# Four graph layers on one core: copies of features and rho's first pass on ScalarE, the loads at the part change in another order, W ahead of the features

## The chip, the core and the metric

The kernel runs on one core of a Trainium2 chip. A core has TensorE (matmuls; PE in the profile, PEld for its weight loads), VectorE (DVE), ScalarE (ACT), GpSimd (POOL) and SyncE (SP), each with an instruction queue of its own, and 16 DMA engines that move the transfers issued by SP, ScalarE and GpSimd. Working memory is SBUF, and matmuls write into eight PSUM banks. The metric is the device time of one execution in microseconds; the comparison is made by the median of several runs.

## What is computed

16 samples `x` of 1024 nodes with 256 features, and one adjacency matrix `adj` of 1024 x 1024 with few non-zero elements per row, pass through four layers, all in float32:

```
# layer 0: scored edges
pre_u, pre_v = h @ W1[:d], h @ W1[d:]
S   = sigmoid(relu(pre_u[:, :, None] + pre_v[:, None] + b1) @ W2 + b2)
a_t = einsum('buv,bud->bvd', S * adj, h)
m_t = einsum('uv,bud->bvd', adj, h) * h
z   = beta1 * h + beta2 * (a_t @ Wa + ba) + beta3 * (m_t @ Wm + bm)
# layer 1
z = z + relu(einsum('ij,bjd->bid', adj, z) @ W.T + b)
# layers 2 and 3, each with weights of its own
feats = z @ W1.T
f1    = feats @ W2 + b2
coefs = softmax(leaky_relu(f1[:, :, None] + f1[:, None, :]) + adj)
z     = coefs @ feats + bias2 + z
```

## The kernel before

**Preparation (to about 111 us).** `load_h` loads a sample, `load_w1` the three pieces of W (both halves of W1, and Wa), and eight loads bring the rows of `adj` into `adj_sb`. The order of the issues is that of lines 378 to 384. ScalarE's DMA queue carries two of the four pieces of sample 0 and then W; SP's queue carries the other two pieces, sample 1, adj, samples 2 and 3. TensorE transposes samples 0 to 3 (L300) and multiplies them with W (`edge_sides`), in the order that `first_group` writes out; ScalarE copies the results into `st` (L323, L324), from where they go to u_d, v_d and hw_d in DRAM. Meanwhile VectorE scales Wa by beta2 (L159) and then finds the largest 32 elements of each row of `adj` (L438 to L444). Three small matmuls (L458, L460, L478) count over partitions what it found; the last of its results, `ok`, decides which arm of the kernel runs (L507). With these inputs it is the arm with lists of neighbours.

**First part (to about 956 us).** For each sample, `messages` multiplies it with `adj`, and `without_edges` makes zb, the part of layer 0 that needs no scores, and stores it as zb_d. Beside it run the scores.

**Scores.** `score_steps` is a generator of 8 steps of search and 152 steps for each group of four samples (608 in all). A step gathers 128 rows of v_d (GpSimd, L697, 0.5 MB), adds u (VectorE, L807), applies relu and the weight (VectorE, L809) and sums over the features in four ScalarE activations (L813). The scores go to DRAM by scatters (L702, `dense_d`). `Side.along` drives it: each `yield` of the main work gives a number of microseconds, times `RATE` (0.26 in the first part, 0.255 after), and for each whole one that is owed a score step is issued. So the yields set how much scoring stands between which pieces of main work. A group's products wait until all of its scores are scattered (`while g not in finished`, and the wait of `load_gd`).

**Second part, by groups of four samples.** `with_edges` runs over four column blocks `v` and eight row tiles `ut` in each. A step loads a 0.5 MB block gd of scores (L888, four buffers, SP's queue), ScalarE reorders it into gc (L1066), and TensorE multiplies hw with it (16 matmul instructions) into all eight banks. After each `v` VectorE adds the sums to `z` (L1089). The z tiles of the first group come from zb_d, 1 MB each (`load_z`, L902); its first four gd blocks are loaded ahead, at the end of the first part. In the first group the same loop reloads the transposed adjacency into `adj_sb` (L1081, 0.5 MB for each of eight rows; it is called `ea` from there on) and takes its exponential on ScalarE (`exponential`, L1056). `paced(ins, n)` makes an instruction wait for the product that was issued n products earlier. An SP queue entry that waits holds up all entries behind it.

`pair_layers` then takes two samples through layers 1 to 3. Layer 1 is `layer_one` (L1106, L1116, L1117, L1124). Layers 2 and 3 factor the softmax: `front` makes the features of a sample in eight tiles, each a matmul into one bank and a copy to SBUF (L982); the copy goes through `evacuate`, which takes VectorE (L136) and ScalarE (L138) in turn. There are 32 fronts (16 samples, two layers). `scales` finds the largest logit (L997 to L1011), makes `rho` in two passes (L1013: add the shift and take the positive part, from two banks of 512 columns; L1016: the exponential), `tau` (L1017), and scales the features (L1018, L1020). It isn't issued at once but put on the list `later`, which `catch_up` empties after the second tile of the next front (L983) or after the first tile of the next `sums`. `sums` makes a tile `m` from rho, tau and ea on VectorE (L1038, four buffers) and multiplies it with the features into four banks; VectorE and ScalarE then divide and write back (L1051, L1212, L1223, or L1249, L1253).

The last group has no scores beside it. Its second pair's layer 1 is instead gathered by lists (`far_ahead`, `by_lists`, `from_lists`) while its first pair runs.

The program is recorded line by line, but the layer beneath it may move instructions of one engine past each other where nothing depends on the order.

Of the kernel before, what the change touches and what calls it, by code (L numbers as in the profile page):

```python
# [12 lines left out]
AF = mybir.ActivationFunctionType  # L13
ALU = mybir.AluOpType
AX = mybir.AxisListType
P = 128
# [22 lines left out]
def after(tc, ins, others, kind, why):  # L39
    dep = mybir.DependencyInfo(kind, mybir.DependencyReason.DATA)  # L40
    for o in others:
        tc.add_manual_dep(ins.ins, o.ins.name, dep, reason=why)
# [23 lines left out]
def gnn_stack_kernel(  # L66
# [27 lines left out]
    nc = tc.nc  # L94
    B, N, D = x.shape
    NT = N // P
    DH = D // P
    HN = 512
# [9 lines left out]
    def bank():  # L108
        return psum[-1].tile([P, HN], F32, tag="bank", name="bank")
# [8 lines left out]
    def paced(ins, back=6):  # L118


        if recent:
            after(tc, ins, [recent[max(0, len(recent) - back)]], mybir.DependencyClass.Sync, "keeps pace")
        return ins

    def product(*args, **kw):
        recent.append(nc.tensor.matmul(*args, **kw))  # L126
        del recent[:-BACK]
        return recent[-1]
# [4 lines left out]
    def evacuate(dst, src):  # L133
        turn[0] += 1
        if turn[0] % 2 and not by_scalar[0]:
            nc.vector.tensor_copy(dst, src)  # L136
        else:
            nc.scalar.activation(dst, src, AF.Copy)  # L138
# [12 lines left out]
    def load_w1(pool, queue):  # L151

        w = pool.tile([P, DH, 3, D], F32, name="w1")
        for s, a in enumerate((g0_W1[:D], g0_W1[D:], g0_Wa)):
            queue.dma_start(w[:, :, s, :], a.rearrange("(c p) k -> p c k", p=P))
        return w

    def with_beta2(w):
        return nc.vector.tensor_scalar(w[:, :, 2, :], w[:, :, 2, :], beta2, None, ALU.mult)  # L159
# [112 lines left out]
        flat = dense[i][:DUMP].rearrange("(c p r) b -> c p (r b)", p=P, r=ZERO // GB)  # L272
        return [flat[c] for c in range(flat.shape[0])]

    def load_h(pool, b, pieces=1, other=nc.sync):
        h = pool.tile([P, NT, D], F32, tag="wide", name="h")
        n = NT // pieces
        for t in range(0, NT, n):
            queue = other if t // n % 2 else nc.sync
            queue.dma_start(h[:, t : t + n, :], x[b, t * P : (t + n) * P].rearrange("(t p) d -> p t d", p=P))  # L280
        return h

    def node_pairs(t):
# [81 lines left out]
    with ExitStack() as stack:  # L365
        prep = stack.enter_context(tc.tile_pool(name="prep", bufs=4))
        prep1 = stack.enter_context(tc.tile_pool(name="prep1", bufs=1))
        early = stack.enter_context(tc.tile_pool(name="early", bufs=8))
# [6 lines left out]
                yield 2.4  # L375
                yield from edge_sides(prep, b, w1, hT)

        hs = [load_h(early, 0, pieces=4, other=nc.scalar)]
        w1 = load_w1(prep1, nc.scalar)
        with_beta2(w1)  # L380
        hs.append(load_h(early, 1))
        for t in range(NT):
            nc.sync.dma_start(adj_sb[:, t, :], adj_v[:, t, :])
        hs += [load_h(early, b) for b in range(2, GB)]
# [72 lines left out]
        ps = bank()  # L457
# [219 lines left out]
    with tc.If(listed > 0) as arm:  # L677
        with ExitStack() as stack:
# [197 lines left out]
            def ttile(name):  # L876
                return wide_t.tile([P, TW], F32, tag="wide", name=name)
# [29 lines left out]
            z_loads = []  # L907
# [61 lines left out]
            to_load, to_exp = list(range(NT)), []  # L969

            def front(x, weights):

                wT = weights.wT
                f = ttile("feats").rearrange("p (t d) -> p t d", t=NT)
                for jt in range(NT):
                    ps = bank()
                    for dh in range(DH):
                        product(
                            ps[:, : D + 1], x[:, dh, jt * P : (jt + 1) * P], wT[:, dh, :],
                            start=dh == 0, stop=dh == DH - 1,  # L980
                        )
                    evacuate(f[:, jt, :], ps[:, : D + 1])  # L982
                    if jt == 1:  # L983
                        catch_up()
                    yield 0.86
                made = {}
                later.append(lambda: scales(f, weights, made))
                return made

            def scales(f, weights, made):  # L990


                b2 = weights.b2
                r = two.tile([P, N], F32, tag="rho", name="rho")
                ta = small.tile([P, NT], F32, tag="tau", name="tau")
                top = small.tile([P, 1], F32, tag="top", name="top")
                nc.vector.tensor_reduce(top, f[:, :, D], AX.X, ALU.max)  # L997
                sh = small.tile([P, 4], F32, tag="shift", name="shift")
                banks = []
                for v in range(NV):  # L1000
                    ps = bank()
                    for c in range(HT):
                        jt = v * HT + c
                        nc.tensor.transpose(  # L1004
                            ps[:, c * P : (c + 1) * P], f[:, jt, D : D + 1].to_broadcast([P, P]), ident
                        )
                    banks.append(ps)
                ps = bank()
                nc.tensor.transpose(ps[:, :P], top.to_broadcast([P, P]), ident)
                nc.vector.tensor_reduce(sh[:, 0:1], ps[:, :P], AX.X, ALU.max)  # L1010
                nc.vector.scalar_tensor_tensor(sh[:, 3:4], b2, 2.0, sh[:, 0:1], ALU.mult, ALU.add)  # L1011
                for v in range(NV):
                    nc.vector.tensor_scalar(r[:, v * HN : (v + 1) * HN], banks[v], sh[:, 3:4], 0.0, ALU.add, ALU.max)  # L1013
                nc.vector.tensor_scalar(sh[:, 1:2], sh[:, 0:1], -0.01, None, ALU.mult)
                nc.vector.tensor_scalar(sh[:, 2:3], sh[:, 0:1], -0.99, None, ALU.mult)
                nc.scalar.activation(r, r, AF.Exp, scale=-0.99)  # L1016
                nc.scalar.activation(ta, f[:, :, D], AF.Exp, bias=sh[:, 2:3], scale=0.99)  # L1017
                nc.scalar.activation(f[:, :, D], f[:, :, D], AF.Exp, bias=sh[:, 1:2], scale=0.01)  # L1018
                for jt in range(NT):
                    nc.scalar.activation(f[:, jt, :D], f[:, jt, :D], AF.Identity, scale=f[:, jt, D : D + 1])  # L1020
                made.update(f=f, r=r, ta=ta)
# [3 lines left out]
            def catch_up():  # L1025
                while later:
                    later.pop(0)()
# [27 lines left out]
            def exponential(jt):  # L1055
                paced(nc.scalar.activation(ea[:, jt, :], ea[:, jt, :], AF.Exp), 16)  # L1056

            def with_edges(g, hw, z):

                for v in range(N // QN):  # L1060
                    cols = slice(v * QN, (v + 1) * QN)
                    acc = [[bank() for _ in range(DH)] for _ in range(GB)]
                    for ut in range(NT):
                        gd = first_gd.pop(0) if first_gd else load_gd(g, v, ut, back=BACK)
                        gc = gc_pool.tile([P, GB, QN], F32, tag="gc", name="gc")
                        paced(nc.scalar.activation(gc, gd.rearrange("p n i -> p i n"), AF.Copy), 16)  # L1066
                        for i in range(GB):
                            for eh in range(DH):
                                product(
                                    acc[i][eh][:, :QN], hw[i][:, ut, eh * P : (eh + 1) * P], gc[:, i, :],  # L1070
                                    start=ut == 0, stop=ut == NT - 1,
                                )
                        if z_loads and ut > 1:
                            load, i = z_loads.pop(0)
                            paced(load(i))
                        if (to_load or to_exp) and ut % 2 and not z_loads:
                            if v and to_exp:
                                exponential(to_exp.pop(0))
                            if to_load:
                                jt = to_load.pop(0)  # L1080
                                paced(nc.sync.dma_start(ea[:, jt, :], adjT_d[jt]), 16)  # L1081
                                to_exp.append(jt)
                        yield 3.4
                    if v == N // QN - 1:
                        while to_exp:
                            exponential(to_exp.pop(0))
                    for i in range(GB):
                        for eh in range(DH):
                            nc.vector.scalar_tensor_tensor(  # L1089
                                z[i][:, eh, cols], acc[i][eh][:, :QN], zbias[:, eh : eh + 1], z[i][:, eh, cols],  # L1090
                                ALU.add, ALU.add,
                            )
# [105 lines left out]
            def pair_layers(b, z, ahead, first):  # L1198
# [59 lines left out]


                m0 = yield from front(z[0], gat2)  # L1260
                m1 = yield from front(z[1], gat2)
                yield from sums(m0, 0, second(0))
# [57 lines left out]
    with arm.Else():  # L1320
        with ExitStack() as stack:
# [88 lines left out]
            with tc.For_i(0, B, 1) as b:  # L1410
                h = load_h(wide, b)
# [36 lines left out]
```

## Time and profile before

| | us |
|---|---|
| median of 3 runs (lowest, highest) | 3244.6 (3230.55, 3249.76) |
| profiled execution: its time, the span of its instructions | 3257.53, 3255.8 |
| TensorE busy, by stage (us from the start of the span): | |
| 300 to 900 (first part) | 596.7 of 600 |
| 900 to 1200 (part change, first products) | 279.5 of 300 |
| 1200 to 2600 (second part, groups 0 to 2) | 1352.4 of 1400 |
| 2600 to 3256 (last group) | 626.1 of 656 |
| TensorE clock granted, mean over the span | 0.988 |

The profile lists every instruction with its start and length, and what ended the idle time of its engine before it. A line such as `PE bank L126 <- DVE m L1038` reads: TensorE's instruction of line 126 that writes `bank` waited for VectorE's instruction of line 1038 that writes `m`. All products are issued by a helper, so they share line 126 and are told apart by their tiles. A float32 product appears as two matmul instructions; matmuls are pipelined, and 64 of 256 columns take 14.1 us at full clock. The groups list the mean time of one instruction, and the waits list total, number and longest. `DMA share` is the mean busy share of the 16 engines and can pass 1 where packets overlap. The execution profiled is 13 us slower than the median of the runs.

### The profile page before, as it was taken

Reading aid. Unit: us, or ns where it says so; the run is one execution under the profiler, and the core shown is the slowest. Engines: PE = TensorE matmul, PEld = TensorE weight load, DVE = VectorE, ACT = ScalarE, POOL = GpSimd, SP = SyncE. Lnnn points to the kernel's source line nnn. Section 1 sums busy time; section 2 is a strip of 40 time slices with the busy share of each in tenths; the row PEclk is TensorE's granted clock in tenths of the full one; section 3 lists DMA queues with packets and bytes.
Section 4 is the critical chain, followed back from the end, with each engine's and each line's share of the span. In section 5 each row is a group of like instructions: output and inputs, shape, how many; then the busy total and the mean of one; then the engine's idle time right before and its main releaser. Section 6 shows DMA issues by size and latency. Waiting matters only on the chain. (4 is left out here: it accounts for less than half of the span.)

```text
span 3255.8 us, 39220 instructions
## 1 busy us (share of the span) xinstructions
PE 3132.2 (96%) x12122; PEld 2203.5 (68%) x12122; DVE 2433.7 (75%) x3366; ACT 1880.1 (58%) x6320; POOL 1826.6 (56%) x1483
## 2 busy tenths in 40 slices
PE   8999999999997999999999999999999999999999
PEld 5544544555556678578776867778686678858888
DVE  7787777777775799799668979867898872148754
ACT  3245556566667766566976656688666654413232
POOL 1146888676664666657566666665676550066600
PEclk9999999999998999999999999999999999999999
DMA  8998898879799755656875575587656525475600
GB/s 286 328 323 305 278 288 267 272 226 275 240 322 317 214 162 162 205 154 209 291 226 174 151 221 154 182 286 232 182 151 210 169 90 168 127 246 142 167 15 27
DMA packets 281899, 687.49 MB, mean 211 GB/s; under 512 B 45184, under 2 KB 137344, under 8 KB 274512
## 3 DMA queue, kind: packets, MB, share of 16 engines
q0 software_dynamic: 128224, 387.80, 41.0%
q1 hardware_dynamic: 125472, 245.45, 22.0%
q10 hardware_dynamic: 27984, 51.65, 4.2%
q8 instruction: 97, 1.59, 0.2%
q14 instruction: 122, 1.00, 0.1%
HBM read 553.45 MB, written 131.32 MB: 210 GB/s over the span
## 5 line engine op out<-in xcount | busy, mean ns | idle before, releaser
L813 ACT ACTIVATE z<-z 128x256 f32<-128x256 f32 x2432 | 978.9, 405 | 702.6 <-DVE z L809 613.4
L807 DVE TENSOR_TENSOR z<-z,u 128x1024 f32<-128x1024 f32 x608 | 739.2, 1220 | 402.9 <-PE bank L126 263.0
L126 PE MATMUL bank<-feats,m 128*128 128x257 f32 x4096 | 926.1, 384 | 30.5 <-DVE m L1038 21.7
L697 POOL DMA_INDIRECT z<-v_d,slot_v x512 | 655.1, 1279 | 471.2 <-ACT z L813 241.6
L126 PEld LDWEIGHTS bank<-feats,m 128*128 128x128 f32 x4096 | 768.4, 191 | 160.1 <-DVE m L1038 28.2
L702 POOL DMA_INDIRECT dense_d<-gt,slot_at x512 | 634.1, 1238 | 198.7 <-issue 139.6
L809 DVE SCALAR_TENSOR_TENSOR z<-z,w2r 128x1024 f32<-128x1024 f32 x608 | 737.9, 1220 | 8.5
L126 PE MATMUL bank<-gc,hw 128*128 128x256 f32 x2048 | 459.3, 385 | 33.1 <-ACT gc L1066 28.4
L126 PEld LDWEIGHTS bank<-gc,hw 128*128 128x128 f32 x2048 | 388.4, 192 | 103.4 <-ACT gc L1066 40.5
L813 ACT ACTIVATION_READ_ACCUMULATOR z<-z 128x1 f32 x2432 | 458.2, 188 | 0.0
L126 PE MATMUL bank<-adj_sb,h 128*128 128x512 f32 x1024 | 442.5, 592 | 2.8 <-ACT st L323 2.6
L1038 DVE SCALAR_TENSOR_TENSOR m<-rho,tau,adj_sb 128x512 f32<-128x512 f32 x512 | 374.3, 744 | 69.7 <-PE bank L126 66.2
L126 PE MATMUL bank<-adjT_in,y 128*128 128x512 f32 (+1 forms) x960 | 401.5, 579 | 5.1 <-DMA adjT_in<-adjT_d 2.6
L126 PEld LDWEIGHTS bank<-adj_sb,h 128*128 128x128 f32 x1024 | 194.3, 190 | 243.1 <-issue 237.7
L126 PE MATMUL bank<-w,hT 128*128 128x512 f32 (+1 forms) x1024 | 337.9, 490 | 10.8 <-DMA w<-in_L_gnn_W_dram 8.7
L126 PEld LDWEIGHTS bank<-adjT_in,y 128*128 128x128 f32 x960 | 181.8, 190 | 220.4 <-issue 207.6
L1066 ACT ACTIVATE gc<-gd 128x1024 f32<-128x1024 f32 x128 | 264.6, 2067 | 92.1 <-PE bank L126 53.9
L126 PEld LDWEIGHTS bank<-w,hT 128*128 128x128 f32 x1024 | 195.7, 192 | 154.8 <-issue 131.5
L126 PE MATMUL bank<-g_wT,z 128*128 128x257 f32 x1024 | 235.9, 385 | 1.1 <-DVE z L1117 0.9
L697 POOL DMA_INDIRECT z<-v_d,x_node x96 | 127.7, 1331 | 175.9 <-ACT z L813 108.1
L126 PEld LDWEIGHTS bank<-g_wT,z 128*128 128x128 f32 x1024 | 194.5, 193 | 32.4 <-issue 3.3
L697 POOL DMA_INDIRECT z<-y_d,slot_v x96 | 107.4, 1119 | 62.5 <-DVE msg L1176 41.7
(162 smaller groups left out, 2385.9 us busy)
## 6 DMA issues: line engine op xcount, KB each, us to landing
gd<-dense_d SPq DMA_DIRECT2D x128, 512.0 KB
dense_d<-zero ACTq DMA_DIRECT2D x64, 512.0 KB
adjT_in<-adjT_d SPq DMA_DIRECT2D x112, 256.0 KB
h<-in_x_dram SPq DMA_DIRECT2D x19, 1024.0 KB
u_d<-st SPq DMA_DIRECT2D x64, 256.0 KB
v_d<-st SPq DMA_DIRECT2D x64, 256.0 KB
hw_d<-st SPq DMA_DIRECT2D x64, 256.0 KB
u<-u_d POOLq DMA_DIRECT2D x32, 512.0 KB
```

Of the source, the lines that this page charges most:

```text
L126: recent.append(nc.tensor.matmul(*args, **kw))
L697: return nc.gpsimd.indirect_dma_start(out=dst, out_offset=None, in_=src[:], in_offset=bass.IndirectOffsetOnAxis(ap=at, axis=0), **how,)
L702: return nc.gpsimd.indirect_dma_start(out=dst[:], out_offset=bass.IndirectOffsetOnAxis(ap=at, axis=0), in_=src, in_offset=None,)
L807: paced(nc.vector.tensor_tensor(z, z, u, ALU.add))
L809: nc.vector.scalar_tensor_tensor(zk, zk, 0.0, w2r[:, None, :].to_broadcast([P, GB, D]), ALU.max, ALU.mult)
L813: nc.scalar.activation(zk[:, c, :], zk[:, c, :], AF.Copy, accum_out=s[:, k, c : c + 1])
L1038: nc.vector.scalar_tensor_tensor(m, r[:, cols], ta[:, jt : jt + 1], ea[:, jt, cols], ALU.max, ALU.mult)
L1066: paced(nc.scalar.activation(gc, gd.rearrange("p n i -> p i n"), AF.Copy), 16)
```

## The change

It has four edits. `front` copies all tiles on ScalarE. `scales` makes rho's first pass on ScalarE with Relu and the shift as its bias. In `with_edges` of the first group, one z is loaded on every second step of v = 0 and waits for the product 12 back instead of 6; adj's rows are loaded from v = 1 on, their exponentials taken from v = 2 on; the steps of v = 0 count 1 us towards the scores instead of 3.4. In the preparation, W's three pieces are issued first on ScalarE's queue, all four pieces of sample 0 go on SP's queue, and VectorE's scaling of Wa is recorded behind the load of sample 1.

```
-    def load_h(pool, b, pieces=1, other=nc.sync):
+    def load_h(pool, b, pieces=1):
...
-            queue = other if t // n % 2 else nc.sync
-            queue.dma_start(h[:, t : t + n, :], x[b, t * P : (t + n) * P].rearrange("(t p) d -> p t d", p=P))
+            nc.sync.dma_start(h[:, t : t + n, :], x[b, t * P : (t + n) * P].rearrange("(t p) d -> p t d", p=P))
...
-        hs = [load_h(early, 0, pieces=4, other=nc.scalar)]
         w1 = load_w1(prep1, nc.scalar)
+        hs = [load_h(early, b, pieces=1 if b else 4) for b in range(2)]
         with_beta2(w1)
-        hs.append(load_h(early, 1))
...
-                    evacuate(f[:, jt, :], ps[:, : D + 1])
+                    nc.scalar.activation(f[:, jt, :], ps[:, : D + 1], AF.Copy)
...
-                    nc.vector.tensor_scalar(r[:, v * HN : (v + 1) * HN], banks[v], sh[:, 3:4], 0.0, ALU.add, ALU.max)
+                    nc.scalar.activation(r[:, v * HN : (v + 1) * HN], banks[v], AF.Relu, bias=sh[:, 3:4])
...
-                        if z_loads and ut > 1:
+                        if z_loads and ut % 2 == 0:
                             load, i = z_loads.pop(0)
-                            paced(load(i))
-                        if (to_load or to_exp) and ut % 2 and not z_loads:
-                            if v and to_exp:
+                            paced(load(i), 12)
+                        if (to_load or to_exp) and ut % 2 and v:
+                            if v > 1 and to_exp:
                                 exponential(to_exp.pop(0))
                             if to_load:
                                 jt = to_load.pop(0)
                                 paced(nc.sync.dma_start(ea[:, jt, :], adjT_d[jt]), 16)
                                 to_exp.append(jt)
-                        yield 3.4
+                        yield 3.4 if g or v else 1
```

By instructions, 128 copies (128 x 257) and 64 passes of rho (128 x 512) move from VectorE to ScalarE; TensorE's and GpSimd's instructions are the same in number.

## The prediction

> **What bounds the kernel now.** I read the page's busy shares first, then the waits of TensorE alone, then windows around every place where TensorE stood idle, then the groups of instructions kept apart by shape.
>
> ```profile
> PE 3132.2 (96%) x12122; PEld 2203.5 (68%) x12122; DVE 2433.7 (75%) x3366; ACT 1880.1 (58%) x6320; POOL 1826.6 (56%) x1483
> ```
>
> TensorE is busy 96% of the span, so a change can win only what TensorE idles (3255.8 - 3132.2 = 124 us) and what it does at a reduced clock. The question for each edit is which piece of that it touches. The waits name three places. First the start (waits of 0 to 25 us):
>
> ```profile
> PE bank L126 <- DMA w<-in_L_gnn_W_dram: 8.7, 1, 8.7
> PE bank L300 <- DMA h<-in_x_dram: 4.5, 1, 4.5
> DVE w L159 <- DMA w<-in_L_gnn_Wa_dram: 20.6, 1, 20.6
> ```
>
> TensorE turns the first sample, then waits 8.7 us for W1; VectorE, whose first instruction scales Wa, starts only at 20.6 us. Second the change from the first part to the second (windows, then timeline; columns of the windows: stretch, length, busy PE, PEld, DVE, ACT, POOL, granted clock, DMA share, GB/s):
>
> ```profile
> 960.00:978.00 18.00, 17.47 (x81) 14.77 (x79) 12.01 (x13) 17.58 (x49) 14.51 (x12) 1.00 1.02 402
> 978.00:993.00 15.00, 0.71 (x3) 0.43 (x2) 0.00 (x0) 2.27 (x2) 7.87 (x8) 0.62 1.03 382
> 993.00:1000.00 7.00, 7.00 (x20) 5.61 (x20) 2.66 (x3) 3.71 (x10) 0.00 (x0) 0.59 0.68 241
> ```
> ```profile
> 964.87 3.77 SPq L902 DMA_DIRECT2D z<-zb_d  x2
> ...
> 972.57 3.91 SPq L902 DMA_DIRECT2D z<-zb_d  x2
> 976.57 1.33 SPq L888 DMA_DIRECT2D gd<-dense_d  x3
> 990.50 2.02 ACT L1066 ACTIVATE gc<-gd 128x1024 f32<-128x1024 f32 x1 [12.82 <-DMA gd<-dense_d]
> ```
>
> Four z loads of 1 MB stand ahead of the next gd on SP's queue, the DMA engines are full (1.02, 1.03), gd lands late, and TensorE idles 14.3 us and then works at half clock to about 999 us. Third the attention stages that run beside the scores (waits of TensorE, 1160 to 2690 us, and two of their windows):
>
> ```profile
> PE bank L126 <- DVE m L1038: 18.6, 18, 2.4
> PE bank L1009 <- DVE top L997: 7.2, 2, 6.1
> ```
> ```profile
> 1160.00:1330.00 170.00, 163.71 (x786) 138.69 (x785) 162.77 (x249) 112.84 (x421) 110.76 (x84) 1.00 0.58 163
> 1740.00:1860.00 120.00, 118.04 (x564) 98.30 (x564) 118.77 (x187) 85.06 (x314) 74.25 (x56) 1.00 0.53 148
> ```
>
> VectorE is 96 to 99% busy there, as full as TensorE; ScalarE is at 66 to 71%. Over six such windows (879 us of the span) TensorE was busy 838.6 us, so 40 us were idle.
>
> **What the Trainium skill says.** "TensorE: Matmul & The Clock Gate", section "What's actually happening": after an idle window of about 3.4 us the clock is halved until activity returns. The trace agrees: 0.50 from 982 to 993 and 0.52 to 999 us, and 0.51 from 21 to 26 us. "DMA: Bandwidth & Descriptors", section "Issuing engines are not separate DMA queues": queues of several engines share the same 16 DMA engines, so moving W to another place saves no bytes, only its turn; share 1.02 on SP's and POOL's transfers together agrees. "VectorE: DVE Perf Modes", section "Why PSUM operands drop a tier": fp32 from PSUM gets no fast mode on VectorE. The rows below agree: VectorE is slower than ScalarE on them.
>
> **The change, part by part.** The rows that price it:
>
> ```profile
> L136 DVE COPY feats<-bank 128x257 f32<-128x257 f32 x128 | 53.0, 418 | 12.8 <-PE bank L126 11.9 <-issue 0.5
> L138 ACT ACTIVATE feats<-bank 128x257 f32<-128x257 f32 x128 | 46.5, 375 | 61.2 <-PE bank L126 54.4 <-issue 4.7 <-PE bank L1004 1.8
> L1013 DVE TENSOR_SCALAR rho<-bank,shift 128x512 f32<-128x512 f32 x64 | 44.9, 742 | 0.0
> L1116 ACT ACTIVATE r<-bank,l1b 128x512 f32<-128x512 f32 x60 | 38.3, 678 | 71.2 <-PE bank L126 39.8 <-DVE msg L1176 26.4 <-DMA out_dram<-st 4.9
> ```
>
> *The start.* The two 256 KB pieces of h leave ScalarE's queue and join SP's, so h's four pieces come one after another; W's three pieces (786 KB) go first on ScalarE's. What TensorE needs before the first edge product is h and W1, what it needs for the second is Wa: 1.05 + 0.79 = 1.84 MB. The windows moved 224 GB/s in the first 10 us and 272 in the next 10, so 1.84 MB are through by about 8.2 us; with 1.5 to 2 us from last packet to release (estimate: the first piece's release came at 4.5 us) about 10. Six of sixteen transposes remain (16 took 3.65 us: 1.4) and one copy (0.6): products start near 12 us, against 16.9 with a second stop until 21.2. That is 5 us, plus some 1.5 of half clock that is done earlier. But TensorE's queue holds three small matmuls (L458, L460, L478) behind VectorE's scan of adj. VectorE runs from 21.0 without a gap to about 97.4 and then waits 2.5 us for them. Its start is now set by adj's first row, which has the same 3.4 MB ahead of it or with it as before (h 0 and 1, W, the row), some 18 us: it gains only 3, and TensorE will wait for it instead. So 3 to 5 at the end of preparation; DMA is then full (1.02 to 1.04 from 120 to 150 us), and the waits of 2.9 and 3.5 us for evacuations near 115 and 155 may grow. **Take 3, from 0 to 6.**
>
> *The part change.* z goes out one MB on every second step (ut 0, 2, 4, 6) instead of four from ut 2 on; the eight adj loads start at v = 1, their exponentials at v = 2; the eight steps of v = 0 count 1 instead of 3.4 towards the scores. gd of step 6 then has two z ahead of it in place of four, and the adj row is gone. Is there enough DMA? A step is 16 matmuls; 64 took 14.09 us, so v = 0 takes 28 us. In it must move: z 4.2 MB, eight gd 4.2, zb 1.05, adjT 0.8, and two gathers of 0.5 MB: 11 MB, or 400 GB/s, what the window above shows as full (402). So the wait shrinks and does not vanish: a late z 3 or gd of v = 1 costs 3 to 6 us. Gained: 14.3 idle plus 3.5 of half clock (7 us at 0.5), minus 3 to 6: **take 12, from 6 to 18.** Fewer scores and no exponential in the first steps leave ScalarE some room in v = 1, where TensorE lost 5 us in pieces of 0.8 waiting for gc: **take 2, from 0 to 5.** SP's order also puts z 0 ahead of the zb store; the store isn't ready by then, so nothing queues for it.
>
> The scores fall behind by 8 x 2.4 x 0.255 = 4.9 steps. Added up from the yields, the last group's scores end 13 steps before its products now and 8 after. The last scatters went out to 2684.9 us, the group's first gd was issued at 2707.0 and TensorE took its product up at about 2718. Five steps are some 19 us: the scatters end near 2704, gd is just in time. **Take -1, from -5 to 0.** The earlier groups have over 20 steps to spare.
>
> *Copies and rho.* VectorE loses 53.0 + 44.9 = 97.9 us over 32 fronts, 3.1 us each. ScalarE gains 46.5 (the L138 row for as many) and 64 x 638 ns (38.3 / 60, the same shape with bias and Relu) = 40.8: 87 us, 2.7 each. 24 of the 32 fronts run beside scores, so VectorE's 73 us come out of stages where it is the tighter engine: 96 to 99% becomes about 88 to 90%. Of the 40 us idle there, those on m, top and the VectorE copies are 28.6, and each longer one brings half clock after it. I take 24 gained with that clock. Against it: in a pair's second front, ScalarE now has both relus (1.3) and four more copies (1.5) beside tau, exponentials and scaling that took it 4.9 us (1173.3 to 1178.2), within the 7 us that the front's matmuls take, and the score activations in the same queue. The banks of that front's copies come free later, and sums' third and fourth accumulators need them: 1 to 2 us of wait in each of eight pairs, take 10 in all. **Net 14, from -10 to 30.** In the last group, VectorE's relief helps the gathers by lists, whose end TensorE awaits at 3086 to 3103 us; POOL and DMA set most of that: **take 1, from 0 to 4.**
>
> Sum: 3 + 12 + 2 - 1 + 14 + 1 = 31 us. The profiled execution took 3257.5 us (span 3255.8); it would become 3226. It lies 13 us above the median of the runs, 3244.6, which becomes **3213**.
>
> **The rivals.** *A, the sum above:* 3202 to 3224. *B, each wait is replaced by another:* z 3 and the gd of v = 1 come late and the fronts' ScalarE queue eats VectorE's relief; 3 + 7 + 4 = 14 us, 3230. For it speaks the 400 GB/s demand; against it ScalarE's 66%. *C, VectorE was the true bound of attention:* nearly all of its 73 us beside scores turn into time of TensorE up to the idle and half clock there, 35 in place of 14, and the last group gives 4: 3189. For it speak 99% windows; against it that the sum of idle is 40. *D, slower:* ScalarE becomes what the fronts wait for. Its in-order queue holds score activations that wait for VectorE (613 us in all in the page's first group), and every copy is now behind them, where half had been on VectorE. The other parts win 17, so a net loss per front of 17 / 32 = 0.53 us cancels them; at 1.8 us per front, with the clock halved after waits of over 3 us, the kernel takes 3244.6 - 17 + 58 = 3285. That z moves without relieving gd, the change not doing what it says, is within B.
>
> **How the numbers follow.** A 0.52, B 0.23, C 0.15, D 0.10. One per cent, about what a measurement tells from no change, is 32 us: faster means under 3212. Half of A and all of C make 0.42 faster; the rest of A and B 0.48 the same; D 0.10 slower. The range leaves out the far part of C and all of D but takes in B with its bounds: 3188 to 3246.
>
> **What would show it.** Right: no wait of over 6 us near 980 us and full clock there; W1 waited for under 4 us at the start; VectorE's windows in attention near 90% and the wait for m at half of 18.6 us. Wrong: the wait named gc or z's final addition with the same sum; TensorE waiting for feats copies (ScalarE) by over 15 us; a new gap before the last group's first product, near 2690 us, by scatters that came late; the preparation still ending at 111 us.

## The result and the profile after

| | before | after |
|---|---|---|
| median of 9 runs each (lowest, highest), us | 3239.9 (3230.5, 3249.8) | 3225.4 (3215.5, 3234.5) |
| ratio after / before, 95% interval | | 0.9958 (0.9939 to 0.9978) |
| profiled execution: span, us | 3255.8 | 3224.0 |
| TensorE idle in the six attention windows (879 us) | 40.4 | 23.2 |

The change gains 14 us of 3240 (7 to 20), real but under the 1% that the prediction called no change. The two spans differ by 31.8 us, more than twice as much: the profile of before is 18 us above its median, that of after stands at its own. In the six experiments below that leave VectorE its full load, TensorE idles 31 to 35 us in the same six windows, not 40; of the idle time that the two traces show as gone, 5 to 9 us were thus probably never the change's.

The page after, the share of each engine:

```profile
PE 3128.0 (97%) x12122; PEld 2205.5 (68%) x12122; DVE 2353.0 (73%) x3174; ACT 1946.6 (60%) x6512; POOL 1816.5 (56%) x1483
```

VectorE has 81 us less and ScalarE 67 us more. The rows of the moved work, by line, out<-in, shape and count, then busy time and mean ns:

```profile
L980 ACT ACTIVATE feats<-bank 128x257 f32<-128x257 f32 x256 | 86.7, 381 | 43.6 <-PE bank L126 41.4 <-issue 1.7
...
L1011 ACT ACTIVATE rho<-bank,shift 128x512 f32<-128x512 f32 x64 | 40.2, 679 | 13.6 <-DVE shift L1012 9.4 <-DVE shift L1009 2.3 <-PE bank L1002 1.2
```

(86.7 - 46.5) + 40.2 = 80 us, against 87 in the prediction. The windows of the part change (stretch, length, busy PE, PEld, DVE, ACT, POOL, clock, DMA share, GB/s):

```profile
960.00:978.00 18.00, 15.67 (x73) 13.50 (x72) 5.17 (x6) 9.37 (x21) 11.37 (x10) 1.00 1.02 373
978.00:993.00 15.00, 12.83 (x60) 11.00 (x59) 5.97 (x13) 10.00 (x13) 2.92 (x3) 1.00 0.99 385
993.00:1000.00 7.00, 6.97 (x32) 5.82 (x32) 4.90 (x4) 6.35 (x10) 1.60 (x1) 1.00 0.76 245
```

Where TensorE had 0.71 us of 15 it has 12.83, and the clock stays at 1.00; two waits of about 2.3 and 2.2 us are left, with the DMA engines as full as before. Attention, two of its windows and the sum over all six:

```profile
1160.00:1330.00 170.00, 167.04 (x799) 141.77 (x799) 155.59 (x227) 124.43 (x461) 113.22 (x84) 1.00 0.57 163
...
1740.00:1860.00 120.00, 119.37 (x576) 100.88 (x576) 115.19 (x170) 89.93 (x335) 76.59 (x59) 1.00 0.56 160
...
sum 879.00, PE 855.80 PEld 728.31 DVE 793.11 ACT 616.75 POOL 551.65; mean PE 142.63 PEld 121.39 DVE 132.18 ACT 102.79 POOL 91.94
```

VectorE is at 90% over the six (793.11 of 879), where it had been at 94% (824.2). TensorE's waits there (total, times, longest, 1160 to 2690 us):

```profile
PE bank L126 <- DVE m L1036: 17.8, 9, 8.1
PE bank L126 <- ACT gc L1064: 6.6, 4, 3.7
...
PE bank L126 <- ACT feats L980: 0.8, 1, 0.8
PE bank L1007 <- DVE top L995: 0.4, 2, 0.2
```

Read this with the same view of before (m 18.6 in 18 pieces, top 7.2). The wait for m has half as many pieces and almost the same sum, because one piece is 8.1 us long. It stands at 2043 us, where before TensorE waited 6.1 us for top. The feared wait for ScalarE's copies is 0.8 us. Last, the start; TensorE's waits to 100 us, then its timeline there:

```profile
PE bank L456 <- DVE full L453: 3.2, 1, 3.2
...
PE bank L476 <- DVE total L478: 1.0, 1, 1.0
```
```profile
94.29 0.61 PE L456 MATMUL bank<-full,below 128*128 128x32 f32 x2 [3.20 <-DVE full L453]
```

W is no longer waited for at all and the first edge product starts at 12.0 us, but VectorE's scan starts at 19.8 (21.0 before), and TensorE now waits for its count.

For what follows, the length of stages read off the timelines, in us, each from one profiled execution. A stage ends at the first product or transpose of the next: preparation; column blocks of `with_edges` by group (E0 to E3); both pairs of a group (P0 to P2). What repeats over several versions counts, single differences of 3 us do not. The first part and the last group's two pairs are left out: they lie between 841 and 851 us and between 419 and 428 us in these profiles, so a gain in one stage need not show in the span of the same profile.

| version | prep | E0 | P0 | E1 | P1 | E2 | P2 | E3 |
|---|---|---|---|---|---|---|---|---|
| before | 111.0 | 137.3 | 455.6 | 123.9 | 459.5 | 122.6 | 462.4 | 110.5 |
| after | 109.6 | 127.9 | 451.9 | 117.5 | 457.4 | 120.1 | 449.9 | 114.3 |
| start alone | 106.2 | 137.4 | 458.2 | 122.6 | 457.6 | 117.9 | 449.6 | 110.5 |
| copies alone | 109.4 | 138.6 | 447.0 | 121.0 | 456.8 | 119.1 | 448.0 | 110.5 |
| loads' order alone | 107.6 | 129.9 | 457.0 | 122.5 | 457.8 | 118.9 | 449.6 | 110.5 |
| 1 us yields alone | 108.4 | 131.2 | 455.6 | 119.3 | 463.9 | 119.8 | 450.9 | 113.5 |
| part change (both) | 110.0 | 126.1 | 455.7 | 118.1 | 464.8 | 118.2 | 450.1 | 114.2 |
| part change, paid back | 106.6 | 124.4 | 460.6 | 122.6 | 457.1 | 119.2 | 449.7 | 110.5 |
| after, full yields | 109.3 | 131.7 | 450.5 | 122.5 | 456.5 | 123.3 | 443.0 | 110.5 |
| the same, no burst | 110.3 | 131.6 | 443.3 | 120.7 | 445.6 | 123.5 | 442.8 | 110.5 |

The 462.4 of before in P2 comes back in no other version that leaves VectorE its load: this is the bulk of what its one profile has too much (12 of 18 us).

### The profile page after: what moved, and what is told of

Read it like the earlier page. It is cut to its first block, busy times and chain, and to the rows that moved or that the text cites. A ratio compares the mean times of both kernels' runs of the same rounds, so it can differ in the third digit from the quotient of the medians.

```text
span 3224.0 us, 39221 instructions
## 1 busy us (share of the span) xinstructions
PE 3128.0 (97%) x12122; PEld 2205.5 (68%) x12122; DVE 2353.0 (73%) x3174; ACT 1946.6 (60%) x6512; POOL 1816.5 (56%) x1483
## 5 line engine op out<-in xcount | busy, mean ns | idle before, releaser
L126 PE MATMUL bank<-feats,m 128*128 128x257 f32 x4096 | 921.3, 383 | 19.3 <-DVE m L1036 17.8
L695 POOL DMA_INDIRECT z<-v_d,slot_v x512 | 637.2, 1244 | 479.9 <-ACT z L811 274.3
L700 POOL DMA_INDIRECT dense_d<-gt,slot_at x512 | 645.9, 1262 | 186.5 <-issue 140.1
```

Source lines behind the costliest of these rows:

```text
L695: return nc.gpsimd.indirect_dma_start(out=dst, out_offset=None, in_=src[:], in_offset=bass.IndirectOffsetOnAxis(ap=at, axis=0), **how,)
L700: return nc.gpsimd.indirect_dma_start(out=dst[:], out_offset=bass.IndirectOffsetOnAxis(ap=at, axis=0), in_=src, in_offset=None,)
```

## The experiments

All ratios are to the kernel before on the same chip, with 95% intervals; 0.001 is 3.2 us.

### One edit at a time

*Copies and rho on ScalarE*, nothing else:

```
-                    evacuate(f[:, jt, :], ps[:, : D + 1])
+                    nc.scalar.activation(f[:, jt, :], ps[:, : D + 1], AF.Copy)
...
-                    nc.vector.tensor_scalar(r[:, v * HN : (v + 1) * HN], banks[v], sh[:, 3:4], 0.0, ALU.add, ALU.max)
+                    nc.scalar.activation(r[:, v * HN : (v + 1) * HN], banks[v], AF.Relu, bias=sh[:, 3:4])
```

> Only the copies of features and rho's first pass move to ScalarE. Theory S (VectorE was the tighter engine of attention, the trace's idle there went from 40.4 to 23.2 us): 10 to 17 us faster than before, VectorE's windows at 90 to 94%, TensorE's idle over the six attention windows near 25 us. Theory P (the whole gain of the change, 14 us, is that of the part change, and the attention stages only look better because the profile of before was 17 us over its median): within 4 us of before, the wait at the part change unchanged near 14 us.

Measured: 0.9969 (0.9955 to 0.9983), 10 us gained.

*Copies alone:* the first of these two lines.

> Only the copies of features go to ScalarE; rho's first pass stays on VectorE. Theory S: half of the relief (53 of 98 us of VectorE), 5 to 9 us faster. Theory P: within 4 us. If the copies behind score activations cost TensorE its banks (the downside priced at 10 us), this is slower than the kernel before by up to 10 us and the wait of TensorE for feats copies passes 10 us.

Measured: 0.9961 (0.9946 to 0.9976), 12.6 us, where 5 to 9 were expected.

*The part change alone*, the loads' order and the yields of `with_edges`:

```
-                        if z_loads and ut > 1:
+                        if z_loads and ut % 2 == 0:
                             load, i = z_loads.pop(0)
-                            paced(load(i))
-                        if (to_load or to_exp) and ut % 2 and not z_loads:
-                            if v and to_exp:
+                            paced(load(i), 12)
+                        if (to_load or to_exp) and ut % 2 and v:
+                            if v > 1 and to_exp:
...
-                        yield 3.4
+                        yield 3.4 if g or v else 1
```

> Only the loads at the part change and the 1 us yields. Theory S: 9 to 13 us gained at the part change, of which some 5 come back because the scores end 5 steps later before the last group: 4 to 8 us faster in all. Theory P: 12 to 16 us faster, nothing comes back. Either way the wait near 980 us is under 6 us and the clock stays full there.

Measured: 0.9998 (0.9986 to 1.0011). Nothing, where both theories expected a gain, and although the trace shows the gap closed: TensorE is busy 15.00 of the 15 us from 978 to 993, and E0 has 126.1 us instead of 137.

*The start alone*, W first, sample 0 on SP's queue, the scaling recorded later:

```
-        hs = [load_h(early, 0, pieces=4, other=nc.scalar)]
         w1 = load_w1(prep1, nc.scalar)
+        hs = [load_h(early, b, pieces=1 if b else 4) for b in range(2)]
         with_beta2(w1)
-        hs.append(load_h(early, 1))
```

> Only W first and sample 0 on SP's queue. Both theories: TensorE's first edge product near 12 us, then TensorE waits 3 to 5 us for VectorE's scan near 91 us, and preparation ends 1 to 2 us earlier than the 111.0 of before: 0 to 3 us faster in all, not to be told from no change. A rival: the whole first part shifts with its start, 8 us faster.

Measured: 1.0004 (0.9993 to 1.0015). Nothing.

So the two relocations to ScalarE carry the change, no gain from the start can be seen, and what the part change gains at its place doesn't come through to the end. What follows asks where it goes, and what in VectorE's relief pays.

### What in VectorE's relief pays

*Rho alone:* the second of the two lines.

> Only rho's first pass moves to ScalarE. If VectorE's load is what attention is paid for (45 us off VectorE, against 53 for the copies that gave 12.6), 8 to 12 us faster. If ScalarE's longer chain in a pair's second front or another order gives it back, within 4 us of before, or slower; both moves together were 2.6 us less than the copies alone, which speaks for this.

Measured: 0.9976 (0.9962 to 0.9990), 7.7 us. Copies 12.6 and rho 7.7 do not add up to the 10 (5.5 to 14.5) of both together. The intervals of the single ones are wide (8 to 17, 3 to 12), but the waits, set side by side further down, point the same way.

*Copies alone, and VectorE's time filled up again.* A maximum over a constant tile, whose result nothing reads, is added to VectorE after every second copy, as many as it lost. It waits for a product of six back, so practically for nothing; the copies stay on ScalarE:

```
-                    evacuate(f[:, jt, :], ps[:, : D + 1])
+                    nc.scalar.activation(f[:, jt, :], ps[:, : D + 1], AF.Copy)
+                    if jt % 2 == 0:
+                        paced(nc.vector.tensor_reduce(filler, b1r, AX.X, ALU.max), 6)
```

> The copies are on ScalarE as in the run of the copies alone, and VectorE gets a reduction of 128 x 256 from SBUF (about 0.42 us) in the place of each of the 128 copies that it lost; its result is used by nothing, and it waits for a product that is three tiles older. If VectorE's load was the cost, the 12.6 us come back: within 4 us of before. If the cost was that VectorE's queue waited for the newest product and held up what stands behind it, 8 to 13 us faster than before, as with the copies alone.

Measured: 1.0008 (0.9996 to 1.0020); the whole gain is gone (by the two ratios the filler costs 15 us). The group of the added work:

```profile
L985 DVE TENSOR_REDUCE filler<-b1r 128x1 f32<-128x256 f32 x128 | 52.3, 409 | 5.8 <-PE bank L126 5.1
```

52.3 us stand in for 53.0 us of copies, and VectorE waited 5.8 us in all ahead of them. So it was not that VectorE's queue stood behind copies which waited for the newest product; its plain load was the cost. TensorE's waits (1160 to 2690 us), first copies alone, then with the filler:

```profile
PE bank L1009 <- DVE top L997: 9.3, 3, 5.6
PE bank L126 <- ACT gc L1066: 7.4, 9, 2.0
PE bank L126 <- DVE m L1038: 5.5, 12, 1.8
```
```profile
PE bank L126 <- DVE m L1041: 16.0, 20, 2.4
PE bank L1012 <- DVE top L1000: 9.4, 3, 6.2
```

The load moves one wait, that for m: 5.5 us without it, 16.0 with it. The wait for top stays at 9.3.

### What the part change gives back

*The order of loads alone:* the part change's diff without its last two lines; the yields stay 3.4.

> Only the order of the z and adj loads changes; the steps of v = 0 keep 3.4 us for the scores. Theory G (the part change's gain of 11 us is real and is given back because the scores, slowed by the 1 us yields, stand 5 steps later beside attention and before the last group): part of the wait stays, 3 to 8 us of it, nothing is given back, 3 to 8 us faster in all, and the last group's products take 110.5 us again instead of 114. Theory N (whatever is gained at the part change is absorbed later by anything that runs beside it): within 3 us of before.

Measured: 0.9994 (0.9985 to 1.0002), 1.9 us and not clear of zero, though E0 is 7.4 us shorter in its trace.

*The yields alone:*

```
-                        yield 3.4
+                        yield 3.4 if g or v else 1
```

> Only the 1 us yields: the scores fall 5 steps behind, the loads keep the old order. Theory G: 2 to 8 us slower, since the wait near 980 us shrinks little (four z still stand ahead of gd) and the later scores cost some 7 us in the second group's attention and 4 us before the last group's products. Theory N: within 3 us of before.

Measured: 1.0010 (1.0001 to 1.0020), 3.2 us slower. The stages show a gain and where it goes: E0 is 6 us shorter and E1 some 3, but P1 is 6 longer (463.9 against 457.6 and 457.8 with the start alone and the loads' order alone; before, whose profile lies 18 us above its median, has 459.5) and E3 3. TensorE's waits in P1 of this version (1655 to 2119 us):

```profile
PE bank L126 <- DVE m L1038: 15.3, 9, 6.0
```

*The part change with the score steps paid back.* The eight yields of 1 us withhold 19.2 us from the scores; the first sixteen yields of the neighbours' products in the first group's first pair give it back, so everything later stands where it stood before:

```
+            owed = [19.2]
...
-                    yield 3.4 * n / HN
+                    back = min(owed[0], 1.2)
+                    owed[0] -= back
+                    yield 3.4 * n / HN + back
```

> Loads and yields of the part change alone, with the same 19.2 us given back in the first pair's layer 1. Theory G: the 11 us gained at the part change are kept, less what loads alone fell short of their stage: 4 to 10 us faster than before, where the part change alone was even. Rival N: within 3 us of before.

Measured: 0.9977 (0.9968 to 0.9985), 7.4 us, where the same part change without this gave 0.9998; the intervals are apart. Its waits in P1 (1661 to 2118 us):

```profile
PE bank L1010 <- DVE top L998: 6.1, 1, 6.1
PE bank L126 <- DVE m L1039: 4.7, 7, 1.3
```

m is back from 15.3 to 4.7 us, top takes its 6.1, E3 is back at 110.5. The give-back is thus the shift of the score steps and not the loads. TensorE's time in P1, without the pay-back and with it (columns as above):

```profile
1654.00:2119.00 465.00, 449.54 (x1866) 337.21 (x1865) 407.06 (x580) 293.72 (x1107) 290.19 (x226) 0.98 0.60 178
1661.00:2118.00 457.00, 444.54 (x1865) 333.95 (x1864) 406.62 (x578) 293.14 (x1106) 297.86 (x224) 0.99 0.62 181
```

Of the 8 us that P1 is longer without it, 3 are idle time and 5 are the same matmuls taking longer, at a lower mean clock. The pay-back has a price too: P0 is 460.6 us with it and 455.7 without.

*The changed kernel with the same pay-back*, and *with full yields*; the second is

```
-                        yield 3.4 if g or v else 1
+                        yield 3.4
```

> The changed kernel, and the 19.2 us that v = 0 withholds from the scores are given back in the sixteen steps of the first pair's layer 1 (1.2 each), where VectorE is at 74% and ScalarE at 59%. Theory G: first products 126 to 128 us, second group's pairs near 454, last group's products 110.5: 17 to 24 us faster than before, the fastest so far. Rival (scores packed into layer 1 slow it as much): like the changed kernel, 10 to 16 us faster than before, with the first group's pairs some 5 us longer.

Measured: 0.9956 (0.9938 to 0.9974).

> The changed kernel, but the steps of v = 0 count 3.4 us towards the scores again. Theory G (the 1 us yields give back in later attention and before the last group what they win at the part change): the first products take 130 us instead of 128, the second group's two pairs 454 instead of 457 to 461, the last group's products 110.5 instead of 114.3; 10 to 18 us faster than before, as fast as the changed kernel or up to 4 us faster. Rival: the yields are what makes the part change pay; then 4 to 8 us slower than the changed kernel, 6 to 10 us faster than before.

Measured: 0.9949 (0.9931 to 0.9968). In both TensorE waits 4.2 to 4.5 us for m instead of 17.8, and E3 is back at 110.5. But the wait for top returns (10.3 and 11.1 us instead of 0.4), the idle time of the six windows falls only from 23.2 to 21.2 and 22.9 us, and neither ratio can be told from the changed kernel's own 0.9958. The 17 to 24 us expected of the pay-back did not come. So on top of the relief of VectorE a give-back is not shown; the intervals leave room for a few us.

### The wait that outlived all of it

Every version so far kept one wait of 5.6 to 8.1 us near 2020 to 2046 us, booked to top or to m. VectorE's timeline in the changed kernel with full yields:

```profile
2018.86 0.77 DVE L1036 SCALAR_TENSOR_TENSOR m<-rho,tau,adj_sb 128x512 f32<-128x512 f32 x1
2028.35 1.23 DVE L805 TENSOR_TENSOR z<-z,u 128x1024 f32<-128x1024 f32 x1 [8.72 <-DMA z<-v_d,slot_v]
2029.49 0.16 DVE L995 TENSOR_REDUCE top<-feats 128x1 f32<-128x8 f32 x1
```

VectorE isn't busy here. It stands 8.72 us at the first instruction of a score step, whose gather is late, and top, which needs nothing of it, stands behind. The same stop is in the kernel before and in the changed kernel:

```profile
2047.42 1.23 DVE L807 TENSOR_TENSOR z<-z,u 128x1024 f32<-128x1024 f32 x1 [7.08 <-DMA z<-v_d,slot_v]
2046.41 1.23 DVE L805 TENSOR_TENSOR z<-z,u 128x1024 f32<-128x1024 f32 x1 [8.19 <-DMA z<-v_d,slot_v]
```

GpSimd's timeline in the execution with full yields says why:

```profile
1997.57 1.26 POOL L695 DMA_INDIRECT z<-v_d,slot_v  x1 [0.30 <-ACT val L1210]
1999.14 1.01 POOL L700 DMA_INDIRECT dense_d<-gt,slot_at  x1 [0.30 <-DVE z L805]
...
2021.45 0.98 POOL L700 DMA_INDIRECT dense_d<-gt,slot_at  x1 [0.30 <-issue]
2022.73 0.97 POOL L700 DMA_INDIRECT dense_d<-gt,slot_at  x1 [0.31 <-issue]
2024.01 0.98 POOL L695 DMA_INDIRECT z<-v_d,slot_v  x1 [0.30 <-issue]
```

From 1999 to 2024 us it issues nothing but scatters, since the end of a group sends all that are still owed in one go. For 25 us no gather goes out. The edit, on top of full yields, keeps the pace of the other scatters at the end of the first three groups (it sends them behind gathers) and counts a group as finished when its last is out:

```
                 waiting = []
+                ending = []
...
                         if t == last_of[g]:
-                            for group, *what in waiting:
-                                group.add(scatter(*what))
-                            waiting.clear()
-                            finished.append(g)
+                            ending.append(g)
+                            for group, *what in waiting if g == NGR - 1 else []:
+                                group.add(scatter(*what))
+                            if g == NGR - 1:
+                                waiting.clear()
+                    while ending and not any(w[0] is put[ending[0]] for w in waiting):
+                        finished.append(ending.pop(0))
```

> In every version so far one wait of 5.6 to 8.1 us near 2020 to 2046 us outlives all relief of VectorE; it is booked to top or to m. Theory Q: VectorE's first instruction of a score step waits there for its gather (17.3 us of such waits in five pieces, the longest 7 to 9), because at the end of a group's scores all scatters still owed (12 or more, 1.3 to 1.8 us each) go out on GpSimd in one go and the next gathers stand behind them. Here, on top of the version with the changed kernel and the full yields, the scatters at the end of the first three groups go out at the pace of all others, behind gathers; only the last group's still go at once. Q expects the waits for top near 1390 (3.6 us) and 2023 (6.5 us) gone, VectorE's waits for the gather under 10 us, and with some half clock a gain of 8 to 12 us over that version's ratio of 0.9949: 0.991 to 0.9925, clear of the changed kernel's own 0.9958. Rival R: the gather is late for another reason (DMA engines, the pace of GpSimd altogether), so the wait stays within 2 us of 6.5 and the ratio is 0.994 to 0.996. Rival S: scatters later than before delay the next group's scores loads or gathers later on: waits for gc before the next group's products or for m grow by what is saved.

Measured: 3198.2 us, 0.9901 (0.9885 to 0.9917), clear of the changed kernel and of before. GpSimd's timeline at the same stretch, then TensorE's waits (1160 to 2690 us):

```profile
2001.99 2.16 POOL L700 DMA_INDIRECT dense_d<-gt,slot_at  x1 [0.31 <-issue]
2004.45 1.50 POOL L695 DMA_INDIRECT z<-v_d,slot_v  x1 [0.30 <-issue]
2006.26 1.08 POOL L700 DMA_INDIRECT dense_d<-gt,slot_at  x1 [0.30 <-issue]
```
```profile
PE bank L126 <- ACT gc L1068: 8.3, 8, 2.0
PE bank L126 <- DVE m L1040: 4.2, 5, 2.4
```

VectorE's waits for a gather from 1000 to 2690 us, with the burst and without it:

```profile
DVE z L805 <- DMA z<-v_d,slot_v: 17.2, 5, 8.7
DVE z L806 <- DMA z<-v_d,slot_v: 0.2, 1, 0.2
```

Gathers now go out between the scatters; the wait for top is gone, that for m is the 4.2 us of before this edit, P0 is 7 and P1 11 us shorter, and no wait of TensorE in these stages has grown. (The first part is 7 us longer in this profile, 851 against 844, within the spread of all versions.) Its gain over full yields, 0.9949 to 0.9901, is 15 us with some 8 of uncertainty either way; the expectation had 8 to 12.

### The wait for VectorE, all versions side by side

Over 1160 to 2690 us (idle: TensorE, six windows), in us. The windows are fixed in time, and the stages in them shift by up to 50 us from version to version, so differences of 1 or 2 us mean nothing; counted over the stages P0 to P2 themselves, TensorE's idle time is within 3 us of the figures here:

| version | m: total, times, longest | top: total | idle | ratio |
|---|---|---|---|---|
| before | 18.6, 18, 2.4 | 7.2 | 40.4 | 1 |
| start alone | 18.3, 19, 2.4 | 6.8 | 32.6 | 1.0004 |
| loads' order alone | 18.4, 19, 2.4 | 7.2 | 34.9 | 0.9994 |
| part change, paid back | 18.4, 19, 2.4 | 7.2 | 34.3 | 0.9977 |
| copies, filled up | 16.0, 20, 2.4 | 9.4 | 31.1 | 1.0008 |
| copies alone | 5.5, 12, 1.8 | 9.3 | 21.2 | 0.9961 |
| rho alone | 5.5, 7, 2.4 | 8.4 | 22.0 | 0.9976 |
| copies and rho | 4.2, 5, 2.4 | 10.0 | 20.7 | 0.9969 |
| 1 us yields alone | 28.9, 24, 6.0 | 0 | 32.0 | 1.0010 |
| part change (both) | 28.9, 24, 6.0 | 0 | 33.7 | 0.9998 |
| after | 17.8, 9, 8.1 | 0.4 | 23.2 | 0.9958 |
| after, paid back | 4.5, 6, 2.4 | 11.1 | 22.9 | 0.9956 |
| after, full yields | 4.2, 5, 2.4 | 10.3 | 21.2 | 0.9949 |
| the same, no burst | 4.2, 5, 2.4 | 0 | 12.9 | 0.9901 |

Either relief takes the wait for m from 18 to 5.5, the second only from 5.5 to 4.2; that fits 12.6 and 7.7 making 10. Against the versions with VectorE's full load (31 to 35 idle) each relief wins 9 to 14 us of idle time; the ratios say 12.6 and 7.7.

## Why the prediction was right, and where its terms were off

The median, 3225.4, lies in the range 12 us above the forecast, and the likeliest of the three outcomes, within 1%, came. That is owed to the width of the range more than to the sum: the sum was 31 us and 14 (7 to 20) came, mostly from the copies and rho (10); start, part change and scores, priced at 16 together, show nothing clear of noise when measured alone (-1 and 0.6). The terms:

- **The start, 3 (0 to 6): measured -1 (-5 to 2).** Its steps held: W1 no longer waited for, the first product at 12.0 (near 12), Wa scaled at 9.2 us (about 10), TensorE waiting for VectorE's scan instead. But the scan gained 1.2 us and not 3, and TensorE's wait for its count came with half clock of its own (0.50 from 94.3 to 100 us). The Trainium skill ("TensorE: Matmul & The Clock Gate", "What's actually happening") puts that after some 3.4 us of idleness; here a wait of 3.2 us, to 94.3 us, was enough. The preparation ended at 109.6 us, not 108; with the start edit alone at 106.2, and without it between 106.6 and 111.0 from one version to the next, so the edit can't be seen in it. The wait for a late transfer was replaced by one for VectorE's scan, and the result can't be told from 0, the low end of the range.
- **The part change, 12 (6 to 18), and 2 for ScalarE's room behind it: right at its place, not in the sum.** E0 is 9.4 us shorter in after and 11 in the part change alone, which with the late scores was priced at 13 and measured 0.6 (-4 to 5); two waits of 2.2 to 2.3 us are left, 4.5 in all, where 3 to 6 was priced; full clock there.
- **The scores 4.9 steps late, -1 (-5 to 0): the step whose reasoning failed.** The sentence "The earlier groups have over 20 steps to spare" looked for a cost only where a group's scores come too late for its products. There the cost was 3.7 us (a wait for gc at 2680.5, E3 114.3 against 110.5). In the part change alone the larger part came in the second group, where no deadline is near: shifted by five steps, the score work meets other products, P1 is 8 us longer, and TensorE waits there for m for 15.3 us (yields alone) instead of 4.7 (paid back). Against that E1 got some 4 us back. That the shift is the cause there is shown by the pay-back (0.9998 to 0.9977, 7 us). In the changed kernel, where VectorE is relieved, the pay-back moves nothing that can be told (0.9958 to 0.9956), so how much of the missing 17 us this step explains stays open. Why P1 suffers is shown only in part: the burst of scatters that holds VectorE falls among products of m instead of in front of top, as the waits for m of 6.0 (yields alone) and 8.1 us (after) near 2045 say; why the shorter waits for m grow as well, by some 5 us, stays open. Open too is why the loads' order alone, with E0 7.4 us shorter, gives no more than 1.9 (at most 4.8) of time; with the score steps kept away from it and paid back later, E0 is 13 us shorter and the gain 7.4.
- **Copies and rho, 14 (-10 to 30): 10 measured (5.5 to 14.5), the right cause, with both halves of the sum wrong.** 24 was taken for m, top and VectorE's copies together with their half clock. m's wait fell further than the forecast half, from 18.6 to 4.2; top's did not fall (7.2 to 10.0), since it isn't VectorE's work that is late there but a gather behind a burst of scatters. The 10 us of waits on ScalarE did not come: feats 0.8 us in after. Rows also counted more than they weigh: 97.9 us of VectorE rows moved, its busy time fell by 80.7, because neighbours on VectorE overlap at their ends (four m in a row take 2.73 us, not 4 x 744 ns; some 0.08 us for each of 192 instructions moved is an estimated 16 of the 17 us). The prediction's 96 to 99% were those of the two windows that it shows, the mean of the six was 94%; "near 90%" held in sum (90%), not in these two (91.5 and 96%).
- **VectorE's relief in the last group, 1 (0 to 4): nothing seen.** The two waits near its end (L1191, L1193 before) are 3.8 and 5.5 us as before (3.5 and 5.5).

Of the rivals, B gave 14 us in sum, as measured, but from other terms (start 3, part 7, fronts 4, where 0, about 0 and 10 came), and the replaced wait was neither z nor gd nor a front's queue. C, VectorE as the full bound, fell: a filler of 52 us costs 13 to 15, not nearly all, and of the 21 us still idle after all relief, 8 went with the burst of scatters. D fell: TensorE waited 0.8 us for ScalarE's copies, and those copies alone made the kernel faster. The place where the Trainium skill would have advised against the edit, "ScalarE: Activation LUTs", "Rules for kernel authors" (relu, max and add belong on VectorE, which it says is faster in bf16), doesn't carry over to these shapes: from PSUM in float32 the pass takes 742 ns on VectorE and 679 on ScalarE, and moving it won 7.7 us.

## What to carry to other kernels

When two engines are both near their limit, relief of the second pays a fraction of what is moved (here 12.6 of 53 us, 7.7 of 45, and 10 of the 98 of both) and pays once: the next relief finds the wait already gone. A change to how side work is metered moves that work everywhere downstream, so price it over the whole span or give the amount back at once. And where a wait survives every relief of the engine it is booked to, read that engine's own timeline: it may itself stand in order behind a transfer, and the cure is in the queue that issues it.

## What was unexpected of the hardware

- An indirect transfer occupies GpSimd's queue for 1.3 to 2.9 us from one issue to the next, gathers and scatters alike: sixteen scatters in a row kept all gathers back for 25 us, although the DMA engines had room (their share was 0.06 to 0.45 in the changed kernel's burst, 2020 to 2047 us). Spreading them was worth about as much as the whole change (15 us, some 8 either way, against 14).
- In the attention windows VectorE was busy for 94 to 95% of the time. While the score steps stood as in before, TensorE had no long wait for m there but some twenty of at most 2.4 us, 16 to 19 us in sum; with 53 us of work less on VectorE they came to 5.5 us.
